# A selective scan beside a dense mixture of experts: turns of four scan steps and four expert slices, with Silu on ScalarE and four scan products summed on GpSimd

## Chip, core and metric

One core of a Trainium2 chip runs the whole program. The metric is the device time of one execution in microseconds; the figure for a kernel is the median of its runs. Four compute engines work in parallel: TensorE (PE, matrix products), VectorE (DVE), ScalarE (ACT) and GpSimd (POOL). SyncE (SP) issues most of the transfers.

## The reference, cut to what matters

The input is x of shape (16, 256, 128), float32, so there are 4096 tokens. The first half is a Mamba block with a small feed-forward part, the second a mixture of eight experts in which every token goes through every expert.

```python
# Mamba (per sequence; D_INNER 256, D_STATE 16)
xi, z = split(layernorm(x) @ in_proj_w.T)
xc    = silu(causal_conv4(xi) + conv_b)
dt, B, C = split(xc @ x_proj_w.T);  dt = softplus(dt @ dt_proj_w.T + dt_proj_b)
A = -exp(A_log)
for t in tokens:                        # h: (256, 16)
    h = exp(dt_t * A) * h + dt_t * B_t * xc_t
    y_t = sum over the 16 states of h * C_t
y = (y + D * xc) * silu(z)
x1 = x + y @ out_proj_w.T
block = x1 + relu(layernorm(x1) @ w1.T + b1) @ w2.T + b2
x2 = layernorm(x + block)
# experts, all eight for every token
acc = sum over e of (silu(x2 @ Wg[e]) * (x2 @ Wu[e])) @ Wd[e]
out = layernorm(x2 + acc)
```

## The kernel before

The 4096 tokens are cut into 8 groups of 512 tokens (two sequences). Channels lie on the 128 partitions and the 512 tokens along the free axis, so nearly every operation is on a 128 x 512 float32 tile, and a matrix product of 128 x 128 with 128 x 512 is recorded as two PE instructions.

The scan of a group is 32 steps: two halves of the 256 channels times 16 states. One step is a `front` and a `back`. `front` makes the decay `dA` with an Exp on ScalarE, written to one of two PSUM banks, and `dBx`, the product of B and u, on GpSimd. `back` runs the recurrence over all 512 tokens as one `tensor_tensor_scan` on VectorE (`dA` is overwritten with h) and multiplies by C into `hC`, also on VectorE. `sum_states` then adds `hC` to y on PE: four 128 x 128 transposes that accumulate into the bank `y`, 16 steps per half, with D * xc (`skip`) as the first term. B and C go out to DRAM once per group (`bc`) and come back broadcast to all partitions, two states per transfer (`fetch`).

The experts of a group are 32 slices: 8 experts times 4 quarters of the 512 hidden units. For a slice, `up` makes two products on PE, `pg` and `pu`; ScalarE makes Tanh of pg/2 and copies `pu` to SBUF (`us`); `half_gate` on VectorE makes (tanh + 1) * pg, which is twice the Silu; `hidden` on GpSimd multiplies by `us`; `down` adds the slice to the bank `acc` on PE. The factor 2 is taken out in `stage_e`. The same form of the Silu is used for `xc` (the convolution's weights are halved in `prepare`) and for `zg`, and the factor is taken out in `stage_c`.

The rest of a group's work is written as Python generators, the stages. `stage_a` and `stage_conv` prepare a group's scan (norm, in-projection, convolution, dt, B, C, z); `gate` and `stage_y` close a half of the scan; `stage_c` does the out-projection, the norms and the feed-forward part and makes `x2T`, the experts' input; `stage_e` closes the experts of a group. Each `yield` is a point at which another piece of work may be written to the queues. `half()` moves all running stages to their next `yield`; `half(quick=True)` moves only those launched as quick.

The schedule is manual: instructions are put into each engine's queue in the order in which the Python code issues them. The main loop issues one scan step and one expert slice per round, and the stages at fixed points between them. The experts work one group behind the scan; in the first rounds, until the first `x2T`, there is a scan alone, and in the last ones there are experts alone. PSUM has 8 banks: two for `dA`, one for `y`, one for `acc`, and four that `grab` and `give` hand round in turn to `pg`, `pu` and the stages. While experts run, the stages together hold at most one of the four (`limit`).

Of the kernel before, what the change touches and what calls it, by code (L numbers as in the profile page):

```python
# [12 lines left out]
P = 128  # L13
L = 256
DM = 128
NH = 2
# [8 lines left out]
NC = 2  # L25
NK = NH * NS
NJ = NE * NF
AHEAD = 2
LAG_Y = 2
LAG_D = 2  # L30
FETCH = 4
START_A = 11
NB = 4
NEARLY = 6
EPS = 1e-5
# [5 lines left out]
def kernel(  # L41
# [110 lines left out]

    def prepare():

        nc.vector.tensor_scalar(cw, cw, 0.5, None, ALU.mult)
        nc.vector.tensor_scalar(cb, cb, 0.5, None, ALU.mult)
        yield
        nc.scalar.activation(A_sb, A_sb, AF.Exp)
        yield
        nc.vector.tensor_scalar(A_sb, A_sb, SLOW, -1.0, ALU.max, ALU.mult)  # L160
        yield
# [63 lines left out]

    def stage_a(g):  # L230
# [49 lines left out]
        for h in range(NH):  # L280
            pv = yield from take(f"pv{g}_{h}")
            nc.tensor.matmul(pv, lhsT=dtw[:, bass.ts(h, P)], rhs=dbc[0:DTR, :], start=True, stop=True)  # L282
            pvs.append(pv)
            if h == 0 and g < 2:
                continue
            yield
            for i, pv in enumerate(pvs, h + 1 - len(pvs)):
                nc.scalar.activation(dt[:, i, :], pv, AF.Identity, bias=dtb[:, i : i + 1])
                done(f"pv{g}_{i}")
            pvs = []  # L290
            if h == 0:
                yield
# [12 lines left out]
        for h in range(NH):  # L305

            pz = yield from take(f"pz{g}_{h}")
            for c in range(NTT):
                nc.tensor.matmul(
                    pz[:, bass.ts(c, P)], lhsT=xn[:, bass.ts(c, P)], rhs=inw[:, bass.ts(NH + h, P)],  # L310
                    start=True, stop=True,
                )
            yield
            tz = wide("tz", f"tz{g}_{h}", 1)
            nc.scalar.activation(tz, pz, AF.Tanh, scale=0.5)
            yield

            nc.vector.scalar_tensor_tensor(zg[:, h, :], tz, 1.0, pz, ALU.add, ALU.mult)
            done(f"pz{g}_{h}")
        yield  # L320

    def stage_conv(g, h, xn):
# [13 lines left out]
        for k in range(1, KC):  # L336
# [4 lines left out]
            if g > 1 and k == KC - 2:  # L341
                yield
                yield
        yield
        nc.scalar.activation(pi, hc, AF.Tanh)
        yield
        nc.vector.scalar_tensor_tensor(s["xc"][:, h, :], pi, 1.0, hc, ALU.add, ALU.mult)
        done(f"pi{g}_{h}")
        s.setdefault("conv", set()).add(h)
        yield  # L350


    def fetch(g, k):
        s = state[g]
        n0 = k % NS
        for what, r0 in (("B", n0), ("C", NS + n0)):
            t = scan.tile([P, NC, TB], FP, tag=what, bufs=3, name=f"{what}{g}_{k}")
            nc.sync.dma_start(out=t, in_=s["bc"][r0 : r0 + NC, :].partition_broadcast(P))
            s[what, k // NC] = t

    def front(g, k):
        s = state[g]
        h, n = divmod(k, NS)
        dA = bank("dA", f"dA{g}_{k}", 2)
        nc.scalar.activation(dA, s["dt"][:, h, :], AF.Exp, scale=A_sb[:, h, n : n + 1])  # L365
        dBx = scan.tile([P, TB], FP, tag="dBx", bufs=4, name=f"dBx{g}_{k}")
        nc.gpsimd.tensor_tensor(dBx, s["B", k // NC][:, k % NC, :], s["u"][:, h, :], ALU.mult)  # L367
        s["front", k] = dA, dBx

    def back(g, k):  # L370
        s = state[g]
        dA, dBx = s.pop(("front", k))
        nc.vector.tensor_tensor_scan(dA, dA, dBx, 0.0, ALU.mult, ALU.add)  # L373
        hC = scan.tile([P, TB], FP, tag="hC", bufs=4, name=f"hC{g}_{k}")
        nc.vector.tensor_mul(hC, dA, s["C", k // NC][:, k % NC, :])  # L375
        s["hC", k] = hC

    def add_transposed(y, src, first, last):
        for c in range(NTT):
# [2 lines left out]
                start=first and c == 0, stop=last and c == NTT - 1, skip_group_check=True,  # L382
            )

    def skip(g, h):
        s = state[g]
        t = s["skip", h] = wide("skip", f"skip{g}_{h}", 1)
        nc.scalar.activation(t, s["xc"][:, h, :], AF.Copy, scale=D_sb[:, h : h + 1])

    def sum_states(g, k):  # L390
        s = state[g]
        h, n = divmod(k, NS)
        if n == 0:
            s["y", h] = bank("y", f"y{g}_{h}")
            add_transposed(s["y", h], s.pop(("skip", h)), True, False)
        add_transposed(s["y", h], s.pop(("hC", k)), False, n == NS - 1)

    def gate(g, h):
        s = state[g]
# [17 lines left out]
    def stage_c(g):  # L417
# [11 lines left out]
        yield  # L429
        yield  # L430
        x1 = wide("x1", f"x1{g}", 1)
        nc.vector.scalar_tensor_tensor(x1, po, 0.5, xtf, ALU.mult, ALU.add)
        done(f"po{g}")
        stats = norm_stats(as4(x1), f"b{g}")

# [59 lines left out]
    def up(g, j):  # L495
        s = state[g]
        e, f = divmod(j, NF)
        pg = grab(f"pg{g}_{j}")
        nc.tensor.matmul(pg, lhsT=wg[:, e, bass.ts(f, P)], rhs=s["x2T"], start=True, stop=True)  # L499
        pu = grab(f"pu{g}_{j}")  # L500
        nc.tensor.matmul(pu, lhsT=wu[:, e, bass.ts(f, P)], rhs=s["x2T"], start=True, stop=True)  # L501
        th = wide("eth", f"eth{g}_{j}", 2)
        nc.scalar.activation(th, pg, AF.Tanh, scale=0.5)  # L503
        us = wide("us", f"us{g}_{j}", 3)
        nc.scalar.copy(us, pu)  # L505
        give(f"pu{g}_{j}")
        s["up", j] = pg, th, us

    def half_gate(g, j):
        s = state[g]  # L510
        pg, th, us = s.pop(("up", j))
        v = wide("v", f"v{g}_{j}", 3)

        nc.vector.scalar_tensor_tensor(v, th, 1.0, pg, ALU.add, ALU.mult)  # L514
        give(f"pg{g}_{j}")
        s["v", j] = v, us

    def hidden(g, j):
        s = state[g]
        v, us = s.pop(("v", j))  # L520
        nc.gpsimd.tensor_tensor(v, v, us, ALU.mult)  # L521
        s["h", j] = v

    def down(g, j):
        s = state[g]
# [7 lines left out]
    def stage_e(g):  # L533
        s = state[g]
        ao = wide("ao", f"ao{g}", 1)
        nc.scalar.mul(ao, s["acc"], 0.5)
        yield
        pt = yield from take(f"pao{g}")
        transpose(pt, as4(ao))
# [12 lines left out]
        yield  # L552


    scans = [(g, k) for g in range(NG) for k in range(NK)]
    slices = []

    running.append([stage_a(0), False])
# [1 line left out]
    while "ready" not in state.get(0, {}):  # L560
# [4 lines left out]
        half()  # L565
        half()
        if "bc" in state[0] and ("B", 0) not in state[0]:
            for k in range(0, FETCH, NC):
                fetch(0, k)
        rounds += 1  # L570
    skip(0, 0)
    for k in range(AHEAD):
        front(0, k)

    t = 0
    j = 0
    queued = 0
    summed = 0
    multiplied = 0
    added = 0  # L580
    while added < NG * NJ or running:
        in_scan = t < len(scans)
        in_experts = j < len(slices)
        limit[0] = 1 if in_experts else NB - 1
        if in_scan:
            g, k = scans[t]
            if k == 0 and 0 < g and g + 1 < NG:
                load_x(g + 1)
            if t in range(NK, NK + NE - NEARLY):
                load_expert(NEARLY + t - NK)  # L590
            if k == START_A and 0 < g and g + 1 < NG:
                running.append([stage_a(g + 1), False])
            t2 = t + FETCH
            if t2 < len(scans) and t2 % NC == 0:
                if "bc" not in state.get(scans[t2][0], {}):
                    raise ValueError("B and C are fetched before they are made")
                fetch(*scans[t2])
        half()
        if in_experts:
            up(*slices[j])  # L600
        half(quick=True)
        half(quick=True)
        lag = LAG_Y if in_experts else 1
        while summed <= min(t - lag, len(scans) - 1):
            gs, ks = scans[summed]
            if ks % NS == 0 and summed:
                gb, kb = scans[summed - 1]
                gate(gb, kb // NS)
                launch(stage_y(gb, 0) if kb // NS == 0 else stage_c(gb), kb // NS == 1)
            sum_states(gs, ks)  # L610
            summed += 1
            if summed == len(scans):
                gate(gs, 1)
                launch(stage_c(gs), True)
        if j > multiplied:
            hidden(*slices[multiplied])
            multiplied += 1
        if in_scan:
            back(g, k)
            t2 = t + AHEAD  # L620
            if t2 < len(scans):
                front(*scans[t2])
                if t2 + 1 < len(scans) and scans[t2 + 1][1] % NS == 0:
                    skip(scans[t2 + 1][0], scans[t2 + 1][1] // NS)
        if in_experts:
            half_gate(*slices[j])
            j += 1
        if added < (multiplied - 1 if in_experts else multiplied):
            gd, jd = slices[added]
            down(gd, jd)  # L630
            added += 1
            if jd == NJ - 1:
                launch(stage_e(gd))
        half()
        if not in_experts:
            half(quick=True)
            half(quick=True)
        if queued < NG and "x2T" in state.get(queued, {}):
            slices += [(queued, n) for n in range(NJ)]
            queued += 1  # L640
        t += 1
# [44 lines left out]
```

## Time and profile before

| | before |
|---|---|
| median of 3 runs | 1087.2 us (1086.2 to 1088.83) |
| the profiled execution | 1086.55 us |
| its span, first to last instruction | 1084.8 us |
| granted PE clock, mean over the span | 0.959 |
| busy, share of the span | PE 91%, DVE 72%, POOL 65%, ACT 59% |
| `x2T` of group 0 is made, experts begin | 135.0 us |
| last scan step | about 947 us |
| a group of 32 steps and 32 slices, in the middle | 122.7 us |

A row of the page's fifth part, or of the list of groups, reads: source line, engine, operation, output <- inputs, shapes, count, then busy time in us and the mean of one in ns, then the idle time of the engine just before these instructions and what ended most of it. A row of the waits reads: who waited, for whom, us in total, how often, the longest. A row of the windows reads: stretch, its length, then the busy us of PE, weight loads, VectorE, ScalarE and GpSimd with their instruction counts, the granted PE clock, and the share and rate of DMA. A row in order of time reads: start, duration, engine, line, operation. The recorded end of a matmul is modelled, and neighbouring matmuls overlap in the record; their starts show their pace.

### The profile page before, as it was taken

To read this page: it belongs to the slowest core of one execution; us is meant where nothing else is said; L and a number is where in the kernel's file an instruction comes from. 1 tells how busy PE (TensorE), PEld (TensorE's weight loads), DVE (VectorE), ACT (ScalarE), POOL (GpSimd) and SP (SyncE) were. 2 spreads that over 40 slices of the span, in tenths; PEclk is the share of its full clock that TensorE was granted. 3 is DMA by queue.
4 is the path that set the end of the run, shared out by engine and by line. 5 is a ranking of instruction groups with operands and counts; after the bars stand their busy time and mean duration, and the time that the engine had idled before them with its cause. 6 is when DMAs were issued, how large, how long until landed. Compare 5 with 4: busy or idle time off the path is not lost.

```text
span 1084.8 us, 11409 instructions
## 1 busy us (share of the span) xinstructions
PE 989.3 (91%) x3488; PEld 517.2 (48%) x3488; DVE 785.6 (72%) x1211; ACT 641.5 (59%) x1091; POOL 710.2 (65%) x591
## 2 busy tenths in 40 slices
PE   4656699997999989999999999999999999999996
PEld 1344455454445544455445544455445545554442
DVE  3798589686978599686978599686987688724222
ACT  4633376754767566765767566755667556544543
POOL 1665477774768577776778577776778678634543
PEclk9755899998999999999999999999999999999999
DMA  8788454443444335443445335343454435100000
GB/s 232 236 264 284 149 169 156 147 144 109 166 157 165 117 117 165 139 146 121 160 158 165 117 116 165 127 158 117 161 156 142 136 117 179 45 0 1 10 1 10
DMA packets 56269, 147.03 MB, mean 136 GB/s; under 512 B 7688, under 2 KB 20880, under 8 KB 56208
## 3 DMA queue, kind: packets, MB, share of 16 engines
q1 hardware_dynamic: 51600, 143.69, 40.4%
q10 hardware_dynamic: 4608, 2.62, 0.8%
q8 instruction: 27, 0.44, 0.2%
q14 instruction: 34, 0.28, 0.1%
HBM read 143.67 MB, written 2.62 MB: 135 GB/s over the span
## 4 chain that ended last, share of the span: by engine, by line
PE 44%; DVE 13%; ACT 3%; issue 2%; POOL 1%; ACTq 0%; POOLq 0%
PE pg L499 11%; PE pu L501 11%; PE acc L529 11%; PE y L380 4%; DVE dA L373 3%; DVE v L514 2%; PE pff L466 2%; PE pf L458 2%; DVE hC L375 2%; ACT x L190 1%; PE po L425 1%; PE pv L282 1%; DVE hc L337 1%; ACT x1h L190 1%; PE pd L267 1%
## 5 line engine op out<-in xcount | busy, mean ns | idle before, releaser
L521 POOL TENSOR_TENSOR v<-v,us 128x512 f32<-128x512 f32 x256 | 324.7, 1269 | 155.8 <-ACT us L505 94.5
L367 POOL TENSOR_TENSOR dBx<-B,u 128x512 f32<-128x512 f32 x256 | 325.0, 1272 | 18.8 <-DMA B<-bc 11.7
L373 DVE TENSOR_TENSOR_SCAN dA<-dA,dBx 128x512 f32<-128x512 f32 x256 | 313.1, 1223 | 0.1
L514 DVE SCALAR_TENSOR_TENSOR v<-eth,pg 128x512 f32<-128x512 f32 x256 | 174.6, 682 | 184.2 <-ACT eth L503 184.1
L499 PE MATMUL pg<-x2T,wg 128*128 128x512 f32 x512 | 265.7, 601 | 0.0
L501 PE MATMUL pu<-x2T,wu 128*128 128x512 f32 x512 | 263.4, 596 | 1.9 <-ACT us L505 1.9
L529 PE MATMUL acc<-v,wd 128*128 128x512 f32 x512 | 262.1, 594 | 1.5 <-POOL v L521 1.5
L503 ACT ACTIVATE eth<-pg 128x512 f32<-128x512 f32 x256 | 152.1, 594 | 163.6 <-PE pg L499 159.9
L365 ACT ACTIVATE dA<-dt,A 128x512 f32<-128x512 f32 x256 | 177.6, 694 | 98.3 <-DVE hC L375 97.8
L380 PEld LDWEIGHTS y<-ident,hC 128*128 128x128 f32 x1024 | 134.4, 151 | 140.7 <-issue 100.6
L380 PE MATMUL y<-ident,hC 128*128 128x128 f32 x1024 | 169.1, 292 | 28.3 <-DVE hC L375 28.2
L375 DVE TENSOR_TENSOR hC<-dA,C 128x512 f32<-128x512 f32 x256 | 176.9, 691 | 10.6
L505 ACT COPY us<-pu 128x512 f32<-128x512 f32 x256 | 149.5, 584 | 55.6 <-PE pu L501 54.4
L501 PEld LDWEIGHTS pu<-x2T,wu 128*128 128x128 f32 x512 | 97.0, 191 | 127.7 <-issue 108.0
L499 PEld LDWEIGHTS pg<-x2T,wg 128*128 128x128 f32 x512 | 92.4, 193 | 100.7 <-issue 72.5
L529 PEld LDWEIGHTS acc<-v,wd 128*128 128x128 f32 x512 | 80.3, 191 | 22.1 <-issue 17.6
L178 POOL TENSOR_TENSOR rs_c<-ve_c,mhalf 128x4 f32<-128x4 f32 x8 | 8.1, 1017 | 69.8 <-DVE ve_c L176 69.8
L337 DVE SCALAR_TENSOR_TENSOR hc<-pi,cw,hc 128x510 f32<-128x510 f32 (+2 forms) x48 | 35.5, 743 | 15.7 <-ACT hc L330 15.0
L297 POOL TENSOR_TENSOR u<-dt,xc 128x512 f32<-128x512 f32 x16 | 20.3, 1271 | 27.5 <-ACT dt L293 27.5
L473 DVE TENSOR_TENSOR res<-pff,res 128x512 f32<-128x512 f32 x8 | 5.5, 692 | 41.9 <-PE pff L466 41.9
L178 POOL TENSOR_TENSOR rs_b<-ve_b,mhalf 128x4 f32<-128x4 f32 x8 | 8.1, 1006 | 41.8 <-DVE ve_b L176 41.8
L458 PE MATMUL pf<-h,w 128*128 128x512 f32 x64 | 33.8, 616 | 0.9 <-ACT h L452 0.9
(84 smaller groups left out, 655.4 us busy)
## 6 DMA issues: line engine op xcount, KB each, us to landing
B<-bc SPq DMA_DIRECT2D x128, 512.0 KB, 4.8
C<-bc SPq DMA_DIRECT2D x128, 512.0 KB, 4.0
xt<-in_x_dram SPq DMA_DIRECT2D x8, 256.0 KB, 4.6
wg<-in_Wg_dram SPq DMA_DIRECT2D x8, 256.0 KB, 6.1
wu<-in_Wu_dram SPq DMA_DIRECT2D x8, 256.0 KB, 5.9
wd<-in_Wd_dram SPq DMA_DIRECT2D x8, 256.0 KB, 6.3
out_dram<-x ACTq DMA_DIRECT2D x8, 256.0 KB, 5.1
bc<-dbc ACTq DMA_DIRECT2D x8, 64.0 KB, 3.0
```

Source lines behind the costliest of these rows:

```text
L365: nc.scalar.activation(dA, s["dt"][:, h, :], AF.Exp, scale=A_sb[:, h, n : n + 1])
L367: nc.gpsimd.tensor_tensor(dBx, s["B", k // NC][:, k % NC, :], s["u"][:, h, :], ALU.mult)
L373: nc.vector.tensor_tensor_scan(dA, dA, dBx, 0.0, ALU.mult, ALU.add)
L375: nc.vector.tensor_mul(hC, dA, s["C", k // NC][:, k % NC, :])
L380: nc.tensor.matmul(y[:, bass.ts(c, P)], lhsT=src[:, bass.ts(c, P)], rhs=ident, is_transpose=True, start=first and c == 0, stop=last and c ...
L499: nc.tensor.matmul(pg, lhsT=wg[:, e, bass.ts(f, P)], rhs=s["x2T"], start=True, stop=True)
L501: nc.tensor.matmul(pu, lhsT=wu[:, e, bass.ts(f, P)], rhs=s["x2T"], start=True, stop=True)
L503: nc.scalar.activation(th, pg, AF.Tanh, scale=0.5)
L505: nc.scalar.copy(us, pu)
L514: nc.vector.scalar_tensor_tensor(v, th, 1.0, pg, ALU.add, ALU.mult)
L521: nc.gpsimd.tensor_tensor(v, v, us, ALU.mult)
L529: nc.tensor.matmul(s["acc"], lhsT=wd[:, e, f, :], rhs=s.pop(("h", j)), start=(j == 0), stop=(j == NJ - 1))
```

## The change

- The Silu is computed as such on ScalarE (`AF.Silu`) for `xc`, `zg` and the expert slices. The Tanh forms go, with their halvings and the factors 0.5 in `prepare`, `stage_c` and `stage_e`.
- Of an expert slice, `up` now makes only `pg` and the Silu into `h`; a new `across` makes `pu` on PE and multiplies it with `h` on VectorE, reading `pu` from PSUM. The copy `us`, `half_gate` and `hidden` go.
- From the second group on, GpSimd adds the `hC` of four steps into one (`fold`, three additions), and PE transposes only that one.
- The main loop is written anew in turns of four steps and four slices. Within a turn the four Silu of the slices follow one another, and then the four Exp. Stages wait with their own Silu for the Silu part of a turn (`silu_time`) while experts run.
- `front` becomes `decay` (Exp, two steps ahead) and `inject` (`dBx`, four steps ahead); `back` becomes `step`. B is fetched eight steps ahead, C four. `dBx` and `hC` have six buffers instead of four.
- `stage_a` of the next group starts at step 4 of a group instead of step 11.

```diff
-AHEAD = 2
-LAG_Y = 2
-LAG_D = 2
-FETCH = 4
-START_A = 11
+NM = 4
+NT = NK // NM
+START_A = 1
...
+    silus = [True]
+
+    def silu_time():
+        while not silus[0]:
+            yield
+            yield
...
-            tz = wide("tz", f"tz{g}_{h}", 1)
-            nc.scalar.activation(tz, pz, AF.Tanh, scale=0.5)
-            yield
-
-            nc.vector.scalar_tensor_tensor(zg[:, h, :], tz, 1.0, pz, ALU.add, ALU.mult)
+            yield from silu_time()
+            nc.scalar.activation(zg[:, h, :], pz, AF.Silu)
...
-        nc.scalar.activation(pi, hc, AF.Tanh)
-        yield
-        nc.vector.scalar_tensor_tensor(s["xc"][:, h, :], pi, 1.0, hc, ALU.add, ALU.mult)
         done(f"pi{g}_{h}")
+        yield
+        yield from silu_time()
+        nc.scalar.activation(s["xc"][:, h, :], hc, AF.Silu)
...
+    def decay(t):
...
+        s["dA", k] = bank("dA", f"dA{g}_{k}", 2)
+        nc.scalar.activation(s["dA", k], s["dt"][:, h, :], AF.Exp, scale=A_sb[:, h, n : n + 1])
...
+    def inject(t):
...
+        nc.gpsimd.tensor_tensor(
+            s["dBx", k], s["B", k // NC][:, k % NC, :], s["u"][:, k // NS, :], ALU.mult
+        )
+
+    def step(t):
...
+        nc.vector.tensor_tensor_scan(dA, dA, s.pop(("dBx", k)), 0.0, ALU.mult, ALU.add)
+        hC = s["hC", k] = scan.tile([P, TB], FP, tag="hC", bufs=6, name=f"hC{g}_{k}")
         nc.vector.tensor_mul(hC, dA, s["C", k // NC][:, k % NC, :])
+
+    def fold(t, other):
+
+        g, k = scans[t]
+        s = state[g]
+        nc.gpsimd.tensor_tensor(s["hC", k], s["hC", k], s["hC", k + other], ALU.add)
...
+    def folded(t):
+        return t >= NK
...
+        s["h", j] = wide("h", f"h{g}_{j}", 6)
+        nc.scalar.activation(s["h", j], pg, AF.Silu)
+        give(f"pg{g}_{j}")
+
+    def across(g, j):
+        s = state[g]
+        e, f = divmod(j, NF)
         pu = grab(f"pu{g}_{j}")
         nc.tensor.matmul(pu, lhsT=wu[:, e, bass.ts(f, P)], rhs=s["x2T"], start=True, stop=True)
-        th = wide("eth", f"eth{g}_{j}", 2)
-        nc.scalar.activation(th, pg, AF.Tanh, scale=0.5)
-        us = wide("us", f"us{g}_{j}", 3)
-        nc.scalar.copy(us, pu)
+        nc.vector.tensor_mul(s["h", j], pu, s["h", j])
         give(f"pu{g}_{j}")
```

The order of a turn, for a group with folds, experts running (t is its first step, j its first slice; the calls are those of the new main loop, with the stage points between them):

```
first part    loads(t); [stages] up(j); up(j+1); down(j-2); down(j-1);
              step(t); fold(t-2, 1); inject(t+4); [quick stages] up(j+2); up(j+3); [stages]
second part   [stages] step(t+1); fold(t-4, 2); inject(t+5); [quick stages]
              across(j); sum_states(t-4); across(j+1); decay(t+2); [stages]
third part    [stages] decay(t+3); loads(t+2); down(j); across(j+2); [quick stages]
              step(t+2); fold(t, 1); inject(t+6); decay(t+4); [stages]
fourth part   [stages] down(j+1); across(j+3); [quick stages]
              step(t+3); inject(t+7); decay(t+5); [stages]
```

The Silu of stages may be issued from the start of a turn until the end of the quick stages of the second part.

## Prediction

> **What bounds the kernel now.** I read the page's busy table, then the windows of one steady group of 32 scan steps, then the order of time inside a plain stretch.
>
> ```profile
> PE 989.3 (91%) x3488; PEld 517.2 (48%) x3488; DVE 785.6 (72%) x1211; ACT 641.5 (59%) x1091; POOL 710.2 (65%) x591
> 621.90:744.60 122.70, 119.23 (x438) 62.08 (x438) 98.31 (x151) 79.41 (x136) 88.50 (x73) 1.00 0.42 142
> ...
> 933.61 1.02 PE L499 MATMUL pg<-x2T,wg 128*128 128x512 f32 x2
> 934.47 1.02 PE L501 MATMUL pu<-x2T,wu 128*128 128x512 f32 x2
> 935.33 0.60 PE L380 MATMUL y<-ident,hC 128*128 128x128 f32 x4
> 935.77 1.02 PE L529 MATMUL acc<-v,wd 128*128 128x512 f32 x2
> 936.63 1.02 PE L499 MATMUL pg<-x2T,wg 128*128 128x512 f32 x2
> ```
>
> In the windows row the five numbers are PE, weight loads, VectorE, ScalarE, GpSimd: PE is busy 119 of 122.7 us at full clock. The ends of matmuls are modelled and overlap, so I take starts: an expert product costs 0.86 us, four transposes 0.44, and step plus slice 3.02 (936.63 - 933.61). Four of them are 12.1 us. The stages add per group, by starts: pf 3.4, pff 3.6, po 1.8, pd 1.8, pv 1.8, pz 1.8, pi 1.7, skip and pyt 1.7, four norm transposes 1.8: 19.4. So PE needs 32 x 3.02 + 19.4 = 116 of the 122.7 us, and 6.7 are stalls. PE is the bound in the 812 us from the first x2T (135.0) to the last scan step (947), 54 turns of four, and in the 128 us of experts alone behind it. The 101 us ahead of it, where group 0 is scanned, are VectorE's.
>
> How the others stand to each other shows here:
>
> ```profile
> DVE v L514 <- ACT eth L503: 184.1, 120, 5.0
> ACT eth L503 <- PE pg L499: 159.9, 161, 4.7
> ACT dA L365 <- DVE hC L375: 97.8, 103, 6.8
> ...
> L503 ACT ACTIVATE eth<-pg 128x512 f32<-128x512 f32 x256 | 152.1, 594 | 163.6 <-PE pg L499 159.9
> L365 ACT ACTIVATE dA<-dt,A 128x512 f32<-128x512 f32 x256 | 177.6, 694 | 98.3 <-DVE hC L375 97.8
> L505 ACT COPY us<-pu 128x512 f32<-128x512 f32 x256 | 149.5, 584 | 55.6 <-PE pu L501 54.4
> L293 ACT ACT_TABLE_LOAD x8 | 10.3, 1283 | 0.1
> L503 ACT ACT_TABLE_LOAD x6 | 7.7, 1283 | 0.1
> ```
>
> VectorE waits for ScalarE, ScalarE for PE: the slack lies there. The third wait is the two dA banks: Exp of step t+2 can't start before step t has ended on VectorE. It stays.
>
> **What the Trainium skill says.** (1) "ScalarE: Activation LUTs", What ACT_TABLE_LOAD costs: 1283 ns for a load, and about 1380 ns of drain beside it. The trace has 1283 ns, but no drain: at Softplus Identity ends at 691.1, the load starts at 691.10, Softplus at 692.39. I take 1.28. (2) Same page, Table sets: exp and tanh share a set; the trace agrees (17 loads beside 256 Exp and 288 Tanh). Silu's set isn't given; I take two loads a turn, as the change words it. (3) Same page: throughput is the same for every function, so Silu is priced as Tanh, 0.59; no row shows a Silu. (4) "GPSIMD Engine Reference", Key points: GpSimd contends with VectorE instructions that have two SBUF inputs. The trace agrees: nb with two such inputs took 1.22 us beside GpSimd work and 0.16 without (at 1079.64). Scan, hC product and the new expert product each read one operand from PSUM, so the folds shouldn't slow them.
>
> **The parts.**
> PE: from step 32 on, three of four transposed sums go: 224 x 3/4 = 168, at 0.44 us 74 us, 10.6 per group. Floor of a group: 116 - 10.6 = 105.4.
> GpSimd: loses 256 v products, gains 168 folds, both at the 1.27 of its rows: -112 us. A turn has 7 operations, 8.9 us, not a bound. The 3 folds precede injections in its queue, but those run 4 steps ahead.
> ScalarE: loses 256 us copies (-149.5); gains two loads in each of 54 turns (+139). As much work, but in bursts: loads can't overlap anything of its own.
> VectorE: v (0.68) becomes the expert product (0.69 like hC: both read PSUM and SBUF); xc and zg products go, 32 x 0.68 = -22 us, and their Tanh becomes a Silu. By starts (52.07, 53.33, 53.94) a scan step takes 1.87 and a product 0.63: 10.0 us a turn.
> SP: as many transfers; B is asked for 8 steps ahead, C 4; each waits for its buffer three pairs back. Landing takes 4 to 5 us, a step 3: hidden; a late one costs at most that.
> Banks, h (6), hC (6): each is handed back a turn earlier than needed, except hC of t+2, which waits for the transposes of t-4; those are 3 us earlier.
>
> **The path of a plain turn.** Each engine works through the order that the program gives it, so I walk the new order from the end of step t-1 (0). ScalarE: Exp t+1 0.69, load 1.28, Silu j 0.59: 2.56. The first pu takes the bank of pg j, so waits for that Silu: 3.4. Then PE waits for the second fold (GpSimd: fold, inject, fold = 3 x 1.27 = 3.8), transposes 0.44, pu 0.86, down 0.86, pu 0.86: 6.9. From a matmul's pace-end to its reader 0.2, VectorE: product 0.63, step t+2 1.87, product 0.63, step t+3 1.87: 12.1, and the next Exp waits there. ScalarE's other leg (three more Silu, load, Exp: 6.3) is ready at step t+2's start. With one bank held by a stage, the fourth pg waits for the first Silu: +0.86 - 0.42 = 12.5. So a plain turn is 12.1 to 12.5 us, against 12.1 before: **the PE time saved in it is idle time**. PE's own work is 12 x 0.86 + 0.44 = 10.8.
>
> So the gain can only come from stage work, which before stood wholly on the bound (19.4 of PE and 6.7 of stalls per group) and now falls into gaps. Of the eight points of a turn where stages advance, the path passes two on each engine. Stage work per group: PE 19.4, ScalarE 22.9 (the group's rows without dA, eth, us), VectorE 17.5: a quarter, 15 us, is on the path. Group: 8 x 12.3 + 15 = 113.4. Waits of in-order engines in the stage chains (norm sums on GpSimd, res on pff) were 6.7; some now meet slack: bounds 0 and 6.7, I take half, 3.4. **Group 116.8, 5.9 less.** In 6.75 groups (54 turns): -40 us.
>
> Around it: in the fill, Silu among the Exps costs up to four pairs of loads at 2 to 3 us, less 2.7 of VectorE products; bounds -3 and +10, I take +3. Experts start only at a turn's end: 0 to 6, inside it. The tail is PE's as before (12 x 0.86 a turn): 0, bounds 0 and +6 for coarser waits. The last v on GpSimd (1.27) becomes a product (0.69): -1.
> Sum: the profiled execution took 1086.55 (span 1084.8 and 1.75 around), 0.65 under the median 1087.2. 1086.6 - 40 + 3 - 1 = 1048.6: **1048 us**. Its own range, with groups of 109 to 121 us and the bounds above: 994 to 1078.
>
> **Rivals.**
> *PE stays the bound.* If the path overlaps better (Silu's table shared with Exp: -2.6 a turn of ScalarE; or stage work wholly in gaps), groups come to PE's 105.4 plus 2: 6.75 x 15.3 = -103, 985 us. For it: PE is now 97% busy. Against: the path above has no queue to run ahead in.
> *The table round trip becomes the bound (slower).* Place: Exp t+1, load, Silu, pu, product, scan, on four in-order engines. Two loads per turn mean that anything a stage puts between them is waited for by all. It decides where more than (122.7 - 98.4)/59.8 = 41% of the stage work lies on the path instead of 25%; with half, a group is 128 us: +38: 1124 us, and 1139 with fill and tail at their upper bounds. For it: ScalarE's stage pieces are long (norm 1.65, conv 0.78, Softplus with its loads), and Silu stages now wait for a Silu phase. Against: half of the stage points lie behind the second load, in ScalarE's slack.
> *GpSimd's folds late.* PE stands at the transposes until the second fold; a norm power behind a late VectorE sum (8.5 us in this group) would hold folds and with them pu: once per group 4 us, 27 us: 1075.
>
> **Numbers.** My forecast with the late folds 0.60, PE the bound 0.18, round trip slower 0.22. A measurement of this kernel tells about 0.2% (2 us) from no change. Faster 0.76, same 0.03, slower 0.21. Range 992 to 1094: it leaves out about half of each rival, 2 in 10.
>
> **What would show it.** x2T copies some 117 us apart (before 122.7); y transposes 352; ACT table loads near 130; PE under 90% busy in a steady group, its waits named by Silu, fold and VectorE; plain turns of 12 to 12.6 us between first pg starts. Wrong if: loads are few; plain turns are under 11.5 (I mislaid the path) or over 13.5; GpSimd is what PE waits for most; the first x2T is past 145.

## The result, and the profile after

The change made the kernel slower: 1127.05 us (median of 4 runs, 1122.26 to 1131.27) against 1088.01 us for the kernel before in the same session (4 runs, 1086.2 to 1089.3). The ratio is 1.0359, with a 95% interval of 1.0309 to 1.0409. The forecast was 1048 us. The profiled execution took 1131.27 us, its span 1129.4 us.

First the page of the kernel after: the busy table, and rows of the costliest groups (the columns are those explained for the profile before; rows left out are marked).

```profile
PE 962.1 (85%) x2816; PEld 458.0 (41%) x2816; DVE 758.5 (67%) x1177; ACT 628.6 (56%) x941; POOL 597.4 (53%) x503
...
L533 DVE TENSOR_TENSOR h<-pu,h 128x512 f32<-128x512 f32 x256 | 176.3, 689 | 278.4 <-PE pu L532 277.9
L400 POOL TENSOR_TENSOR hC<-hC,hC 128x512 f32<-128x512 f32 x168 | 213.3, 1270 | 231.8 <-DVE hC L394 227.4
L525 ACT ACTIVATE h<-pg 128x512 f32<-128x512 f32 x256 | 139.7, 599 | 86.9 <-PE pg L523 85.9
...
L373 ACT ACT_TABLE_LOAD x57 | 73.1, 1283 | 2.8 <-ACT x L187 1.8
L525 ACT ACT_TABLE_LOAD x42 | 53.9, 1283 | 0.7
```

Every engine has less to do than before: PE has 672 instructions fewer, GpSimd is busy 112.8 us less. The parts cost what their rows promised. A fold takes 1.27 us, an expert product 0.69, a Silu 0.599 where a Tanh took 0.594; beside the folds the scan and the product with C keep their 1.22 and 0.69. Only one thing is new on ScalarE, the loads of tables: 123 in all with those of the stages, where the kernel before had 17.

The windows row of a middle group, from one copy of `x2T` to the next (PE, weight loads, VectorE, ScalarE, GpSimd, then the clock):

```profile
528.60:655.50 126.90, 112.29 (x342) 52.75 (x341) 94.07 (x147) 80.00 (x120) 78.18 (x66) 0.99 0.40 138
```

PE issues 96 instructions fewer than in the group of before, and the group still takes 126.9 us instead of 122.7. No engine fills it: PE, the busiest, is at 88%. The list of waits says what stands between them:

```profile
ACT dA L373 <- DVE hC L394: 278.4, 131, 6.2
DVE h L533 <- PE pu L532: 277.9, 174, 6.3
POOL hC L400 <- DVE hC L394: 227.4, 54, 9.2
PEld pu L532 <- ACT h L525: 45.7, 32, 2.8
PEld y L404 <- POOL hC L400: 32.4, 28, 3.3
```

Before, VectorE waited for ScalarE and ScalarE for PE, down a line that ended at the engine that was the bound. Now it is a ring. VectorE waits for PE's `pu`, PE for ScalarE's Silu and GpSimd's folds, and these two for VectorE's scan. No member of the ring can run ahead.

Where the 44.7 us between the two profiled executions went can be read off the copies of `x2T`:

| stretch | before | after | difference |
|---|---|---|---|
| start to the first `x2T` | 135.0 | 140.1 | +5.1 |
| the seven distances between `x2T` | 849.3 | 889.8 | +40.5 |
| last `x2T` to the end of the span | 100.5 | 99.5 | -1.0 |

The whole loss but for the fill lies in the groups: 133.4, 128.1, 127.0, 126.9, 129.9, 128.7 and, for the last, 115.8 us. The two of 129 to 130 us were run at a mean granted clock of 0.96 instead of 0.99, and their PE time is 2 to 3 us longer. The record of the clock says how: it stands at 1.00 or at 0.50, and inside the groups the halves come in stretches of 3.4 us or twice that. A group of 127 us holds one such stretch, one of 129.9 holds three (10.2 us). The windows rows of a whole group of the second kind, and of the inside of its long stretch:

```profile
655.50:785.40 129.90, 115.29 (x342) 53.95 (x341) 94.32 (x147) 80.02 (x120) 78.19 (x66) 0.96 0.40 134
681.40:688.10 6.70, 5.96 (x10) 1.84 (x10) 1.41 (x3) 2.01 (x3) 5.58 (x5) 0.50 0.70 188
```

The middle groups of the kernel before hold none. Between its first and its last `x2T` the kernel after spends 60 us at half clock, the kernel before 11. Turns with and without a stretch differ by 1.3 to 1.7 us (e6 below shows a pair), so an estimate, if it costs as much everywhere, is that 19 to 25 of the 40.5 us go with the clock. The rest is there at full clock too, and even a group with a single stretch is 4.2 us longer than before. In the experiments, then, groups are compared with groups that hold as many stretches.

Inside a group one turn is plain, with no stage work between its instructions. Rows from the order of time of the kernel after, the others left out:

```profile
598.20 0.69 ACT L373 ACTIVATE dA<-dt,A 128x512 f32<-128x512 f32 x1 [1.84 <-DVE hC L394]
598.31 1.26 POOL L400 TENSOR_TENSOR hC<-hC,hC 128x512 f32<-128x512 f32 x1 [5.10 <-DVE hC L394]
598.91 1.28 ACT L525 ACT_TABLE_LOAD   x1
600.20 2.06 ACT L525 ACTIVATE h<-pg 128x512 f32<-128x512 f32 x4
600.76 1.27 POOL L400 TENSOR_TENSOR hC<-hC,hC 128x512 f32<-128x512 f32 x1
600.85 1.12 PE L532 MATMUL pu<-x2T,wu 128*128 128x512 f32 x2 [0.94 <-ACT h L525]
602.08 0.66 PE L404 MATMUL y<-ident,hC 128*128 128x128 f32 x4
602.57 1.02 PE L532 MATMUL pu<-x2T,wu 128*128 128x512 f32 x2
603.43 1.02 PE L541 MATMUL acc<-h,wd 128*128 128x512 f32 x2
604.29 1.02 PE L532 MATMUL pu<-x2T,wu 128*128 128x512 f32 x2
605.35 0.69 DVE L533 TENSOR_TENSOR h<-pu,h 128x512 f32<-128x512 f32 x1 [1.02 <-PE pu L532]
605.96 1.22 DVE L392 TENSOR_TENSOR_SCAN dA<-dA,dBx 128x512 f32<-128x512 f32 x1
611.18 1.28 ACT L525 ACT_TABLE_LOAD   x1
```

From load to load it is 611.18 - 598.91 = 12.27 us. Read down: Exp, load, Silu; the first `pu` waits 0.94 us for that Silu; the transposes of the sum; `pu`, a down product, `pu`; then VectorE's third product, which has waited 1.02 us for its `pu`, and only then the scan of step t+2 (605.96). Two chains run into the transposes side by side. ScalarE's (Exp, load, Silu, first `pu`) ends at 601.71, by the pace of 0.86 us for a `pu`; GpSimd's (fold, injection, fold) ends at 600.76 + 1.27 = 602.03. They are 0.3 us apart.

### The profile page after: what moved, and what is told of

Its sections match the earlier page's. It is cut to its first block, busy times and chain, and to the rows that moved or that the text cites. A ratio compares the mean times of both kernels' runs of the same rounds, so it can differ in the third digit from the quotient of the medians.

```text
span 1129.4 us, 9496 instructions
## 1 busy us (share of the span) xinstructions
PE 962.1 (85%) x2816; PEld 458.0 (41%) x2816; DVE 758.5 (67%) x1177; ACT 628.6 (56%) x941; POOL 597.4 (53%) x503
## 4 chain that ended last, share of the span: by engine, by line
PE 34%; DVE 20%; POOL 9%; ACT 9%; issue 4%; DVEq 0%; POOLq 0%
PE pu L532 12%; DVE dA L392 9%; PE acc L541 7%; PE pg L523 6%; POOL hC L400 5%; DVE hC L394 4%; PE y L404 3%; DVE h L533 3%; POOL dBx L384 2%; PE pff L490 2%; ACT dA L373 2%; PE pf L482 2%; ACT L525 1%; PE pd L273 1%; ACT x L187 1%
## 5 line engine op out<-in xcount | busy, mean ns | idle before, releaser
L533 DVE TENSOR_TENSOR h<-pu,h 128x512 f32<-128x512 f32 x256 | 176.3, 689 | 278.4 <-PE pu L532 277.9
L400 POOL TENSOR_TENSOR hC<-hC,hC 128x512 f32<-128x512 f32 x168 | 213.3, 1270 | 231.8 <-DVE hC L394 227.4
L384 POOL TENSOR_TENSOR dBx<-B,u 128x512 f32<-128x512 f32 x256 | 322.2, 1269 | 19.2 <-DVE dA L392 17.5
L532 PE MATMUL pu<-x2T,wu 128*128 128x512 f32 x512 | 274.6, 622 | 23.1 <-ACT h L525 23.1
L523 PE MATMUL pg<-x2T,wg 128*128 128x512 f32 x512 | 247.8, 603 | 24.1 <-ACT zg L323 10.1
L541 PE MATMUL acc<-h,wd 128*128 128x512 f32 x512 | 254.4, 598 | 1.1 <-DVE h L533 0.9
L525 ACT ACTIVATE h<-pg 128x512 f32<-128x512 f32 x256 | 139.7, 599 | 86.9 <-PE pg L523 85.9
L541 PEld LDWEIGHTS acc<-h,wd 128*128 128x128 f32 x512 | 93.5, 190 | 121.0 <-issue 89.7
L404 PE MATMUL y<-ident,hC 128*128 128x128 f32 x352 | 72.2, 342 | 39.1 <-DVE hC L394 26.0
L404 PEld LDWEIGHTS y<-ident,hC 128*128 128x128 f32 x352 | 50.7, 173 | 82.8 <-DVE hC L394 39.1
L373 ACT ACT_TABLE_LOAD x57 | 73.1, 1283 | 2.8 <-ACT x L187 1.8
L525 ACT ACT_TABLE_LOAD x42 | 53.9, 1283 | 0.7
L484 ACT ACTIVATE r<-pf,fb 128x512 f32<-128x512 f32 x32 | 21.8, 681 | 26.4 <-PE pf L482 26.4
```

The source lines that it names most:

```text
L373: nc.scalar.activation(s["dA", k], s["dt"][:, h, :], AF.Exp, scale=A_sb[:, h, n : n + 1])
L384: nc.gpsimd.tensor_tensor(s["dBx", k], s["B", k // NC][:, k % NC, :], s["u"][:, k // NS, :], ALU.mult)
L400: nc.gpsimd.tensor_tensor(s["hC", k], s["hC", k], s["hC", k + other], ALU.add)
L404: nc.tensor.matmul(y[:, bass.ts(c, P)], lhsT=src[:, bass.ts(c, P)], rhs=ident, is_transpose=True, start=first and c == 0, stop=last and c ...
L525: nc.scalar.activation(s["h", j], pg, AF.Silu)
L533: nc.vector.tensor_mul(s["h", j], pu, s["h", j])
```

## The experiments

A turn's length is the distance between the first scans of two turns. "Group" is the distance between copies of `x2T` in the middle of the run, whatever the clock. Ratios are to the kernel before on the same chip, with their 95% intervals.

| kernel | us | ratio | plain turn | group |
|---|---|---|---|---|
| after | 1127.05 | 1.0359 (1.0309 to 1.0409) | 12.27 | 127 to 130 |
| e1: without Silu's loads | 1108.64 | 1.0195 (1.0178 to 1.0212) | 12.28 | 126.7 |
| e4: sum two `pu` later | 1089.27 | 1.0000 (0.9986 to 1.0015) | 11.7 | 119 to 124 |
| e14: both | 1068.14 | 0.9825 (0.9807 to 0.9842) | 11.6 | 119 to 121 |
| e2: without folds | 1164.75 | 1.0712 (1.0694 to 1.0729) | | 133 to 137 |
| e3: before, with folds of four | 1113.87 | 1.0239 (1.0221 to 1.0258) | | 124 to 127 |
| e3b: before, with folds of two | 1080.12 | 0.9936 (0.9916 to 0.9956) | | 121 to 123 |
| e5: `pu` a turn behind its Silu | 1205.87 | 1.1079 (1.1063 to 1.1096) | 12.2 | 138 to 143 |
| e6: sum and downs behind `pu` | 1054.34 | 0.9678 (0.9657 to 0.9700) | 10.73 | 115.5 to 117.2 |
| e9: e6 without Silu's loads | 1034.01 | 0.9522 (0.9505 to 0.9539) | 10.74 | 115.8 |
| e7: after, stage points later | 1170.93 | 1.0771 (1.0737 to 1.0806) | 12.27 | 134 to 136 |
| e8: e6, stage points later | 1088.90 | 1.0018 (1.0007 to 1.0029) | 10.75 | 122 to 123 |
| e10: after, no feed-forward products | 1103.72 | 1.0164 (1.0131 to 1.0196) | 12.27 | 121 to 126 |
| e11: before, no feed-forward products | 1029.25 | 0.9471 (0.9456 to 0.9487) | | 115.6 |
| e12: after, two norm passes out | 1110.12 | 1.0229 (1.0196 to 1.0262) | 12.27 | 127 to 130 |
| e13: after, convolution taps out | 1111.32 | 1.0219 (1.0189 to 1.0249) | 12.27 | 126.1 |

**Loads or the order of PE?** The theory was the rival of the prediction: the round trip with its two loads. The other suspect was the wait for folds.

```diff
 e1, e14:
-        nc.scalar.activation(s["h", j], pg, AF.Silu)
+        nc.scalar.activation(s["h", j], pg, AF.Tanh)     # and so for xc and zg
 e4, e14:
             across(*slices[j])
-        if fold_last:
-            sum_states(t - NM)
         if in_experts:
             across(*slices[j + 1])
 ...
             lower()
             across(*slices[j + 1])          # third part
+        if fold_last:
+            sum_states(t - NM)
```

> The changed kernel with Tanh in the place of every Silu, so Tanh and Exp need no table load between them; the values of the gates are Tanh's, the work is otherwise the same. Round trip (the loads and the stage work lie on the chain Exp, load, Silu, pu, product, scan): the first load of a turn leaves the chain, 54 x 1.3 us, and up to both with the stage turns, 54 x 2.6: 985 to 1057 us. Late folds (PE waits at the transposes until GpSimd's second fold, which ends 3.9 us after a turn's start whatever ScalarE does): the fold takes the load's place, plain turns stay at 12.0 to 12.3 us, 1085 to 1125.

> The changed kernel with the transposes of the last turn's sum issued two products later on PE (behind the third pu). Late folds: the wait (0.4 us in a plain turn, up to 3.3 in a stage turn) and the 0.44 of the transposes leave the way to the second pu: 0.86 x 54 = 46 us and some more in stage turns, 1060 to 1080 us. Round trip alone: the fold was never the cause, at most 20 us less, 1105 to 1127.

> Both edits together: Tanh for Silu (no loads; the gates' values are Tanh's) and the transposes behind the third pu. If loads and folds are two chains of nearly one length, side by side, each alone gives little and both together give much: plain turns near PE's own 10.8 us, 985 to 1040 us. If only one of them counts, this is no faster than that one alone by more than 20 us.

Without the loads the plain turn stays at 12.28 us. In the order of time of e1 the reason stands in brackets:

```profile
460.10 1.27 POOL L400 TENSOR_TENSOR hC<-hC,hC 128x512 f32<-128x512 f32 x1 [3.63 <-DVE hC L394]
462.55 1.27 POOL L400 TENSOR_TENSOR hC<-hC,hC 128x512 f32<-128x512 f32 x1
463.87 0.66 PE L404 MATMUL y<-ident,hC 128*128 128x128 f32 x4 [1.32 <-POOL hC L400]
465.43 0.69 DVE L533 TENSOR_TENSOR h<-pu,h 128x512 f32<-128x512 f32 x1 [1.02 <-PE pu L532]
```

PE now comes to the transposes early and stands there 1.32 us until the second fold, with three `pu` queued behind. The load had been covered by the folds, and the folds all but 0.3 us by the load. The loads' 18 us (e1 against after) are saved elsewhere: 6.2 lie in the fill (first `x2T` at 133.9 instead of 140.1), and in each group two turns with stage work are shorter, 12.27 instead of 13.67 us and 14.90 instead of 15.18, 1.7 together. The length of e1's groups hides this, since they hold two stretches of half clock where those of after hold one or three. The 38 us of e4 are larger, and both together give 59: the two nearly add. e4 fell between its two expected outcomes, and e14 fell short of its own: 1068 us and a plain turn of 11.6, not 10.8. Loads are a cost, then, but not the largest.

**Is the fold itself the loss?**

```diff
 e2:   def folded(t):
-        return t >= NK
+        return False
 e3, e3b, in the kernel before, before each step's front:
+            fold(*scans[t - 1])     # GpSimd adds pairs (e3b), or pairs and pairs of pairs (e3)
```

> The changed kernel without the folds: PE transposes all four products of a turn, as in the first group. GpSimd loses 168 additions (213 us), PE gains 168 x 0.44 = 74 us. Late folds: PE waits less for GpSimd, but works 1.3 us more in a turn: 1110 to 1140 us. Round trip: the fold was no cause and the additional transposes stand partly between the pu products: 1140 to 1195 us. PE as the bound would give 1127 + 74 = 1200.

> The kernel before with the fold part of the change alone: from the second group on GpSimd adds the products of four steps into one, PE transposes only that (hC six buffers). PE loses 74 us, GpSimd gains 213 (26.7 in a group). If PE alone were the bound of the kernel before: 1088 - 74 = 1014 us. GpSimd then has 88.5 + 26.7 = 115 us in a group besides its waits (15 before), so it becomes the bound at 117 to 124 us a group: 1055 to 1100 us.

> The kernel before with folds of two steps only: GpSimd gains 112 additions x 1.27 = 142 us (20.3 in a group), PE loses 112 x 0.44 = 49 us. Both engines then have 109 us in a group: 112 to 118 us with their waits, 1020 to 1060 us. If GpSimd's waits for VectorE and ScalarE grow with its load, it is GpSimd's again: 1065 to 1100.

Within the new turns the folds are worth 38 us (e2). Added to the kernel before, folds of four make it slower. Its windows row of a middle group, and two of its waits:

```profile
621.00:744.00 123.00, 112.34 (x336) 53.05 (x334) 95.36 (x149) 77.76 (x134) 115.84 (x96) 0.97 0.42 142
```

```profile
PEld acc L545 <- POOL v L537: 67.3, 90, 2.1
PEld y L381 <- POOL hC L411: 55.8, 38, 6.0
```

GpSimd is busy 115.8 of 123 us there, because it still makes the expert products `v`, and PE waits for it. Folds of two leave it room and gain 0.6%. So folds of four pay here only together with the move of the product to VectorE.

**Does it help to break the ring by a whole turn?**

```diff
 e5, in the second part:
-            across(*slices[j])
+        cross(); cross()            # pu and product of the turn before
+            up(*slices[j + 2]); up(*slices[j + 3])
 ...
+        cross(); lower(); cross(); lower()
```

> The changed kernel with pu and the product of a slice one turn behind its Silu (h has eight buffers, dBx five): pu no longer waits for a Silu of its own turn, the transposes stand behind the second pair of pg. Round trip: the leg load, Silu, pu leaves the chain; what binds is PE (10.8) or the two loads around the Silu with two scan steps behind (0.7 + 1.3 + 2.3 + 1.3 + 0.7 + 1.9 + 1.9 = 10.1): plain turns near 11, 1040 to 1075 us. If the chain through ScalarE isn't what holds stage turns, no better than the late sum: 1080 to 1095.

This missed entirely: 1205.87 us, the slowest of all. Two lines of it, the first from the order of time, the second from the waits:

```profile
629.43 0.60 ACT L525 ACTIVATE h<-pg 128x512 f32<-128x512 f32 x1 [1.46 <-PE pg L523]
```

```profile
POOL dBx L384 <- DVE dA L392: 181.1, 75, 7.7
```

No `pu` waits for a Silu of its own turn any more, but the second pair of `pg` now stands behind a pair of `pu`, so the second pair of Silu, the load and the next Exp come later, and all four expert products stand ahead of step t+2 on VectorE. The room for eight `h` was taken from `dBx` (five buffers instead of six), and GpSimd waits 181 us for them. Besides, it spends 138 us at half clock between its first and its last `x2T`, where the kernel after has 60. Which of these weighs most was not taken apart.

**What if PE gives VectorE its `pu` first?** The same products in the same turn, only PE's order changed:

```diff
 e6, as e4, and in the third and the fourth part:
             j += 1
-            lower()
             across(*slices[j + 1])
+            lower()
```

> The changed kernel with the transposes behind the third pu (as in the run with the late sum, 1089 us) and besides each of the third and fourth pu ahead of a down product instead of behind it, so that no down stands between the pu products that VectorE waits for. Order of the turn on the chain: a plain turn goes from 11.7 to about 10.8 us, where PE's own work and the second load bind together: 54 x 0.9 = 49 us, 1040 us; 1050 to 1065 if turns with stage work gain only half of it. If what is left is only the stage work, whatever the order of the products: 1078 to 1090.

1054.34 us, 3.2% faster than the kernel before (ratio 0.9678) and 6.5% faster than the kernel after. Windows, waits and a plain turn of it:

```profile
501.30:616.80 115.50, 109.36 (x342) 52.90 (x341) 94.69 (x147) 79.83 (x120) 78.24 (x66) 1.00 0.43 152
```

```profile
ACT dA L373 <- DVE hC L394: 212.5, 125, 4.0
DVE h L533 <- PE pu L532: 178.7, 157, 6.6
```

```profile
448.05 2.74 PE L532 MATMUL pu<-x2T,wu 128*128 128x512 f32 x6
449.31 1.28 ACT L373 ACT_TABLE_LOAD   x1
449.97 0.69 DVE L533 TENSOR_TENSOR h<-pu,h 128x512 f32<-128x512 f32 x1 [0.17 <-PE pu L532]
450.63 1.02 PE L541 MATMUL acc<-h,wd 128*128 128x512 f32 x2
451.44 1.22 DVE L392 TENSOR_TENSOR_SCAN dA<-dA,dBx 128x512 f32<-128x512 f32 x1
451.49 0.60 PE L404 MATMUL y<-ident,hC 128*128 128x128 f32 x4
```

Three `pu` leave PE back to back, VectorE waits only 0.17 us for the second, and the scan of step t+2 starts just as PE comes to the transposes. With the loads in place the plain turn is 10.73 us; that is PE's own work of a turn, 12 x 0.86 + 0.44 = 10.8. VectorE's wait for `pu` fell from 277.9 to 178.7 us. The 1.5 us that went from a plain turn were due to the order in which PE took its work, to no single operation.

Three of e6's four middle groups hold no stretch of half clock and take 115.5 to 115.9 us; the fourth holds one and takes 117.2. All of the difference lies in one turn, here in a group without and in the one with it:

```profile
355.06:372.25 17.19, 15.72 (x57) 8.19 (x56) 11.87 (x25) 11.04 (x21) 13.07 (x11) 1.00 0.28 96
470.57:489.45 18.88, 17.41 (x57) 8.78 (x56) 12.62 (x24) 11.23 (x21) 13.07 (x11) 0.91 0.23 86
```

> The kernel e6_downlate with Tanh in the place of every Silu, so that some 120 table loads of 1.28 us go (the values are then those of Tanh; the instructions are otherwise the same). Theory: in e6 PE's own work bounds a plain turn, and the loads lie beside it: plain turns unchanged at 10.7 us, a gain from the stage turns alone, 1040 to 1052 us. Rival: the loads are still on the chain in the turns with stage work, two in each of some 40 such turns at half their length: 1.28 x 40 = 51 us, 1000 to 1030 us.

e9 then shows what the loads are worth once that order is mended: 20 us, of which 8.3 lie in the fill (first `x2T` at 132.5 instead of 140.8) and 6.6 in the two groups behind it. In the middle a group with one stretch of half clock takes 115.8 us without the loads and 117.2 with them, a group with none 114.1 and 115.5: 1.4 us, in two turns with stage work (11.57 instead of 12.53, 11.94 instead of 12.39). Both theories of that run were off. The plain turns stayed, as the first said, but the gain is larger than it allowed, mostly by the fill. The rival was right that stage turns pay for loads, but with 1.4 us per group, some 10 in all, where it had put 51.

**How much of the stage work lies on the chain?** A group is eight turns. Eight plain turns of the kernel after are 98.2 us, so the stages put 126.9 - 98.2 = 28.7 us on it. First their place: each part's opening stage point moved behind its scan step.

```diff
 e7 (and e8, on e6), in each of the four parts:
-        half()
 ...
         inject(...)             # third and fourth part: ahead of it
+        half()
```

> The kernel after, with the opening stage point of each of the four parts of a turn moved behind that part's own scan step and injection; the order of PE's sums and downs is as in the kernel after. Theory A (of the 127 us of a steady group 28.7 are stage work on the chain, because the stage points at the head of a part put their instructions ahead of the step, the pg and pu that the next engine waits for): behind the step the same work stands where its engine has just handed over, and part of it goes: groups of 119 to 123, 1085 to 1110 us, plain turns unchanged at 12.2 to 12.4. Theory B (the excess comes from the lengths of the stage chains themselves, and of work that in-order engines must do wherever it stands): groups within 2 of 127, 1115 to 1140 us. Third possibility: the stages' own pace falls because two neighbouring points now lie close together and a stage piece meets its predecessor unfinished: groups over 130, above 1145 us.

> The kernel e6_downlate with the same move of the four opening stage points as e7_stagelate. In e6 a plain turn is PE's own work (10.7 us), and 19.4 of its 30 us of stage excess per group are stage work of PE itself, which no placing removes. Theory A (head-of-part stage points delay the chain): 2 to 6 us less per group, 1015 to 1042 us. Theory B (PE is the bound; placing is nothing): 1048 to 1060 us. If the stages' pieces meet their predecessors unfinished: above 1065 us.

In both kernels the third outcome came true: the same instructions, no plain turn longer, and a group 6 to 7 us longer on after (measured between plain turns: 133.9 against 126.9 with one stretch of half clock, 136.2 against 129.8 with three) and about 6 longer on e6 (121.2 against 115.5 with none). So the 28.7 us are no fixed share of the stage work; they depend on where the points stand. Whether it is because pieces now meet their unfinished predecessors, as that expectation had it, was not taken apart.

Then their content, one piece taken out at a time, with the stage points kept:

```diff
 e10, e11:  pf, Relu and pff left out
-        nc.vector.tensor_add(res, po, res)
+        nc.vector.tensor_add(res, h2, res)
 e12:       the passes xh and x1h left out
-        norm_apply(as4(x1), as4(xh), scale)
-        transpose(pt, as4(xh))
+        transpose(pt, as4(x1))               # and so for xt
 e13:       the taps k = 1 to 3 of the convolution left out
-            nc.vector.scalar_tensor_tensor(hv[:, :, k:], pv[:, :, : L - k], ...)
```

> The kernel after without the two products of the feed-forward part (pf, Relu, pff left out, the stage points kept; res gets h2 in place of pff). By starts that is 3.4 + 3.6 = 7.0 us of PE and 2.7 us of ScalarE per group, 9.7 of the 59.8 us of stage work. If a quarter of stage work lies on the chain, as the prediction had it: 2.4 us less per group, some 1108. If half: 4.7, some 1094. If each piece lies on it wholly, since the chain of waits of a group names pff and pf with 6.3 us: 7 or more, 1070 to 1080.

> The kernel before with the same part left out. The prediction took stage work there as wholly on the bound, PE: 7.0 us less in each of 7.8 groups, 1030 to 1036. If part of it falls in gaps also there: 1045 to 1065.

> The kernel after without the application of two of the four norms (the Identity passes xh and x1h on ScalarE; the transposes read the raw tiles; the sums and powers of the norms stay). 3.2 us of ScalarE per group. A quarter on the chain: 0.8 per group, 1121. Half: 1.6, 1116. Wholly: 3.2, 1104. More than wholly (a piece of ScalarE between load and Silu is waited for, and with it the stage's next piece comes a point earlier): below 1100.

> The kernel after without the six products of the convolution's other taps on VectorE (4.5 us per group in the groups of the trace; stage points kept). Counted between the plain turns of the middle groups, where e10 lost 4.9 of PE's 7.0 us and e12 nothing of ScalarE's 3.2. If VectorE's stage pieces lie on the chain like PE's: 2 to 3.2 us less per group, groups near 126. If wholly: 4.5, groups near 124. If not: 128 to 129.

Between the plain turns of the middle groups, those with as many stretches of half clock compared. "On the chain" is the time that these pieces have, in one such group, in the chain of work that ended last, followed back from the end of the trace:

| taken out | per group | on the chain | kernel | group becomes | lost |
|---|---|---|---|---|---|
| feed-forward products | PE 7.0, ScalarE 2.7 | 7.0 | before (no stretch) | 122.7 to 115.6 | 7.1 |
| the same | PE 7.0, ScalarE 2.7 | 6.3 | after (one) | 126.9 to 124.3 | 2.6 |
| convolution taps | VectorE 4.5 | 1.8 | after (one) | 126.9 to 126.1 | 0.8 |
| two norm passes | ScalarE 3.2 | none | after (one; three) | 126.9; 129.9 | none |

In the kernel before PE's piece lay wholly on the bound: 7.1 us for 7.0. In the kernel after 2.6 remain, and this number isn't clean, as the next paragraph shows. VectorE's piece counts with less than a fifth, ScalarE's pass with nothing. Of the 13.9 us between the profiled executions of after and e12, 5.4 lie in the fill and 6.4 in the last distance between `x2T`; its total fell between what was expected for "half" and for "wholly", and neither is what happened in the middle.

The 4.9 us that e13's expectation names for e10 are a mean of four groups, whatever their clock, and one of them is no like group. In it e10's program makes `x2T` a turn later than that of after, so that one turn runs without experts. From the order of time of its PE:

```profile
400.28 1.12 PE L528 MATMUL acc<-h,wd 128*128 128x512 f32 x2 [0.47 <-DVE h L520]
...
415.77 5.39 PE L510 MATMUL pg<-x2T,wg 128*128 128x512 f32 x8
```

Between these two PE has no expert product. The four slices were left for the end: the last `x2T` of e10 was 38.6 us earlier than that of after, but the experts behind it took 110.0 us instead of 99.5, and the kernel gained only 23 us. In the groups behind, `x2T` stays a turn later, so their 2.6 us stand for the products and for this shift together.

The traced chain spends 31.5 us of one group of after (471.2 to 598.1) on stage work, which is all but the lines of `dA`, `dBx`, `hC`, `y`, `pg`, `pu`, `h` and `acc`: PE 10.7, ScalarE 8.2, VectorE 7.1, GpSimd 5.5. Some of its pieces, as start, duration and what:

```profile
499.27 1.02 POOL rs_b L175
500.29 1.24 POOL res L461
515.00 3.71 PE pff L490 x32
```

It names the pieces that count: the two norm passes aren't on it and gave nothing, the taps and the products are. On the engine that was the bound before, a piece gave back what it had on the chain; in the ring of after less, so other chains end close behind.

## Why the prediction was wrong

- "plain turn 12.1 to 12.5 us": right, 12.27, and by the very chain that was walked. "The PE time saved in it is idle time" is right as well.
- "a quarter, 15 us, is on the path": **this step failed**, together with its companion "I take half, 3.4". They put 18.4 us of stage work and waits into a group; measured were 28.7, or 48% of the 59.8 us (some 1.5 of it by the one stretch of half clock). "Group 116.8, 5.9 less" became 126.9. Over the seven distances between `x2T` the sum had -40 us and the trace +40.5; everything else in it together misses by 2 us. The quarter came from counting stage points, as if each microsecond of stage work had the same chance to meet slack. What the runs show in its place: the traced chain of such a group holds 31.5 us of stage work, twice the 15, unevenly spread: `pf` and `pff` with 6.3 us of their 7.0 of PE, two norm passes with none of their 3.2. The 31.5 hold 5.5 us of GpSimd, which the list of 19.4, 22.9 and 17.5 us left out, though its stage work stands in one queue with the folds; only the late-fold rival touches it. And the same pieces at other points cost 6 to 7 us more. In the kernel before stage work cost 122.7 - 8 x 12.1 = 26 us per group; the change saved no plain turn and made that 28.7. Why the pieces fall as they do was not taken apart further.
- The clock, a term that the sum doesn't have: by the estimate above, 19 to 25 us of the +40.5 go with stretches at half clock. Without them the groups would still be far from 116.8.
- The slower rival: its time, 1124 us for half the stage work on the path and a group of 128, is what came out, and its boundary of 41% was passed; that the time fits so well is in part luck, since the clock is in it, which the rival didn't have. Its mechanism holds in part. The ring Exp, load, Silu, `pu`, product, scan is there, but loads are the smaller part: 18 us without changing PE's order (e1, still slower than before), and 1.4 to 1.7 us of a steady group, whatever the order.
- The late-fold rival: its place was right, its price in plain turns was hidden all but 0.3 us, since ScalarE's chain with the load ends almost as late. It shows openly in e1. In the turn with the late norm power GpSimd does wait, by this line of after:

```profile
550.49 1.02 POOL L175 TENSOR_TENSOR rs_e<-ve_e,mhalf 128x4 f32<-128x4 f32 x1 [6.95 <-DVE ve_e L173]
...
555.26 1.11 PE L404 MATMUL y<-ident,hC 128*128 128x128 f32 x4 [2.51 <-POOL hC L400]
```

  and PE stands at the transposes 2.51 us, where I had priced 4.
- The fill, "I take +3" with bounds -3 and +10: +5.1. The tail and the last product, 0 and -1: -1.0.
- The parts: y transposes 352 and 123 loads as said; GpSimd no bound. On the Trainium skill, "ScalarE: Activation LUTs", What ACT_TABLE_LOAD costs: its price of 1283 ns held in all the loads. Its drain of about 1380 ns didn't show: in the plain turn the Exp begins at 598.20, the load at 598.91 and the Silu at 600.20.
- What I overlooked: I walked the path of the new plain turn and took its order as given. The walk itself named "transposes, `pu`, down, `pu`" ahead of VectorE's product, and 10.8 us as PE's own work. The 1.3 us between them were in my own sum, and no rival was made of them.
- Slips that shift no conclusion: the walk's 6.9 adds up to 6.8; the last scan step begins at 941.9, not 947; and the bounds, added straight, give 990 to 1090 us, not 994 to 1078.

## What to carry to other kernels

When a change takes the work off the engine that was the bound, walk the ring that is left, and look on each in-order engine for work that nobody waits for standing ahead of work that somebody does: here moving sums and downs behind the `pu` products was worth 73 us, nearly twice the loss of the change (an estimate of 12 to 16 of them by less half clock: 29 us between the first and the last `x2T` instead of 60). Don't spread stage work over a chain by a uniform share; ask of each piece, on every engine, what is queued behind it, and if a share must stand in for that, let the range reach from none to all. Where a trace exists, follow its chain: the pieces that weren't on it gave nothing when they were taken out. Test suspects singly and together, here 18 and 38 us alone and 59 together. Before groups are compared, look whether their clock was the same: here one stretch at half clock made 1.3 to 1.7 us.

## What was not expected of the hardware

PE's granted clock is either 1.00 or 0.50 in these records, and a stretch of 3.4 us at half clock, which a mean of 0.96 or 0.99 over a group hides, lengthens a group by 1.3 to 1.7 us. With three of them instead of one PE's busy time for 342 instructions went from 112.3 to 115.3 us and the group from 126.9 to 129.9. The mean clock of the whole span was 0.959 before, 0.929 after and 0.898 in e5, the slowest kernel; but e6, faster than all of these, has 0.936, so the clock doesn't order the kernels, and what sets it was not tested.
